# A pass over the finished instruction list moves some 60 early operations, and the last unit is finished chunk by chunk (attention + expert FFN, one core)

## The chip, the cores and the metric

One core of one Trainium2 chip runs the kernel. The metric is device time in microseconds (us) of one execution, lower is better. Engines are named as in the profile: PE (TensorE matmul; PEld its weight loads), DVE (VectorE), ACT (ScalarE), POOL (GpSimd), SP (the queue that issues the DMAs).

## The reference

x has 8 batches of 512 tokens with 256 features, all in float32. Two sandwiched layers:

```
x = x + layernorm(attn(layernorm(x)))
x = x + layernorm(ffn(layernorm(x)))

attn:  x_proj = x @ w_in.T + b_in           # 16 heads of 16
       att = softmax(q k.T / 4)             # per head, 512 x 512
       opt = einsum('blmh,blhd->blhd', att, v)
       return opt @ w_out.T + b_out
ffn:   top1 = argmax(softmax(x @ gate_W.T + gate_b))       # of 8 experts
       inter = relu(x @ wi_W.T + wi_b + lora_top1(x))      # 1024 wide, rank 4
       return inter @ wo_W.T + wo_b
```

In `opt` the sum over m concerns att alone, so the weights of each row add up to about one: what stays of a head is v times a factor from the row sums. The kernel still forms every score, its row maximum and its exponentials' sum.

## The kernel before, in words

**Precision.** float32 products are made of three matmuls on split operands: `three` (L463) multiplies high by high, high by low and low by high parts. Every operand is therefore split into a rounded high part and the rest: `split` (L297, L299, L301 the high part, L305 the low part) and, out of PSUM, `split_ps` (L360 and L382 on ACT, L367 and L373 on DVE).

**Tiles and stages.** A batch is four chunks of 128 tokens; two chunks make a unit, so there are 16 units. For a batch: `layernorm` (L390: bn_stats L397 and bn_aggr L402 on DVE; nr, the inverse deviation, on POOL at L410 and L415; the apply at L437 on POOL or L439 on DVE), transposes on PE (L454), split into xnh and xnl (L506, L513), then `project` (L520) for groups 0 and 1 of eight heads, queries and keys, into PSUM tiles psqk and from there into hl. `lay_out_k` (L543, DMAs at L556 into `rows`) and `lay_out_q` (L563, DMAs at L577 for the first unit of batch 0, L590 elsewhere) spread hl over partitions for pairs of heads. `scores` (L602) makes for each pair, chunk and head one 128x512 product (L635 for batch 0's first unit, with 64 rows; L626 elsewhere), its negative row maximum nmax on DVE (L645) and exp with row sums on ACT (L654). Five PSUM tiles hold scores. `values`, `attend` and `feed` (L908) follow per unit: v, output projection, layernorm, gate and experts, the FFN's psh and psz, and at the end z, its layernorm, the residual and the output DMA (L976, L397 to L439, L984, L989).

**What sets the order.** Nothing is emitted where it is written. `Plan.op` (L69) records each operation with an engine, a cost and the tiles it reads and writes; `Plan.order` (L103) runs a list scheduler over them with the due times in `WIN` and `PRI`, and at L1156 the finished list is emitted. Each engine then works through its own part of that list strictly in order; semaphores between engines follow from the tiles. SP's DMAs reuse eight semaphores in turn, so a DMA waits until the one eight places earlier has landed.

**What the change touches.** At the start: the x loads (L268) and weight loads (L283) on SP, four of them for wo; `warm_up` (L1009), 100 matmuls of ones into the tile psu (L1016); `first_weights` (L1043: wqk split, and bqk scaled at L1062); the layernorm of batch 0 on DVE (ln_x, L439); the weight splits wv, wout, wi, wo on POOL (L321, L297 and L305); the layernorms of batches 1 to 3 (st_x, mv_x on DVE, nr_x and ln_x on POOL); `gate_weights` (L1089: wga L1093 and L1098, lbh L1111, lbs L1116). In the list before, PE runs 46 psu, the transposes of batch 0 with 2 psu between, 20 psu, the projections and values of batch 0, 23 psu, four scores, 9 psu, and then the scores. At the end: the last unit (batch 7, chunks 2 and 3), whose layernorm and residual run on DVE (`QUICK`).

Of the kernel before, what the change touches and what calls it, by code (L numbers as in the profile page):

```python
# [17 lines left out]
P = 128  # L18
# [30 lines left out]


class Op:
    __slots__ = ("eng", "cost", "share", "lag", "fn", "urgency", "tiles", "after", "deps", "ready", "n", "group")


class Plan:
# [10 lines left out]
    def op(self, eng, cost, fn, reads=(), writes=(), holds=(), share=1.0, lag=0.0, behind=()):  # L66

        o = Op()  # L70
        o.eng, o.cost, o.share, o.lag = eng, cost, share, lag
        o.fn, o.n = fn, len(self.ops)
        o.urgency = self.at
        o.group = None
        deps = set(behind)
        for t in reads:
            deps.update(t.writers)
        for t in writes:
            deps.update(t.readers)
        deps.discard(o)  # L80
        o.deps, o.after, o.ready = len(deps), [], 0.0
        for d in deps:
            d.after.append(o)
        for t in reads:
            t.readers.append(o)
        for t in writes:
            t.writers.append(o)
        o.tiles = list(dict.fromkeys([*reads, *writes, *holds]))
        for t in o.tiles:
            t.left += 1  # L90
        self.ops.append(o)
        return o
# [89 lines left out]
def kernel(  # L182
# [59 lines left out]
    def mm(n, times=1):  # L242
        return (max(n / 2.208, 108) + 2.5) * times
# [3 lines left out]
    def const_tile(shape, dtype, name, parts=1):  # L247
        return plan.tile(const, shape, dtype, name, 1, name)
# [83 lines left out]

    ident = const_tile([P, P], F32, "ident")
    plan.op(POOL, 500, lambda: make_identity(nc, ident()), writes=[ident])
    mhalf = const_tile([P, NC], F32, "mhalf")
    fill(mhalf, -0.5)

# [49 lines left out]
                ({"B": POOL, "D": DVE, "F": ACT}[how], POOL),  # L387
            )

    def layernorm(src, sel, n, pool_, tag, bufs, name, eng=POOL, at_once=None):  # L390

        m = at_once or n
        st = plan.tile(small, [P, n, nc.vector.BN_STATS_DIM], F32, "st", 4, f"st_{name}", False)
        mv = plan.tile(small, [P, n, nc.vector.BN_AGGR_DIM], F32, "mv", 4, f"mv_{name}", False)
        for c in range(n):
            plan.op(
                DVE, 335, lambda c=c: nc.vector.bn_stats(st()[:, c, :], sel()[:, c, :]),  # L397
                reads=[src], writes=[st],
            )
        for c in range(n):  # L400
            plan.op(
                DVE, 75, lambda c=c: nc.vector.bn_aggr(mv()[:, c, :], st()[:, c, :]),  # L402
                reads=[st], writes=[mv],
            )
        few = HOW["few"]
        fe = {POOL: nc.gpsimd, DVE: nc.vector}[few]
        nr = plan.tile(small, [P, 2, n], F32, "nr", 4, f"nr_{name}", False)
        plan.op(
            few, 235 if few == POOL else 70,
            lambda: fe.tensor_scalar(nr()[:, 1, :], mv()[:, :, 1], 1.0, EPS, ALU.mult, ALU.add),  # L410
            reads=[mv], writes=[nr],
        )
        state[0].setdefault("stats", plan.op(
            POOL, 355 + 165 * n,
            lambda: nc.gpsimd.tensor_tensor(  # L415
                nr()[:, 1, :], nr()[:, 1, :], mhalf()[:, :n], ALU.pow
            ),
            reads=[nr, mhalf], writes=[nr],
        ))
        if eng == POOL:  # L420
            plan.op(
                few, 235 if few == POOL else 70,
                lambda: fe.tensor_scalar(
                    nr()[:, 0, :], mv()[:, :, 0], -1.0, 0.0, ALU.mult, ALU.add
                ),
                reads=[mv], writes=[nr],
            )
        e = nc.gpsimd if eng == POOL else nc.vector
        dsts = []
        for c0 in range(0, n, m):  # L430
            dst = plan.tile(pool_, [P, m, D], F32, tag, bufs, f"ln_{name}_{c0}")
            for c in range(c0, c0 + m):
                def apply(c=c, dst=dst, c0=c0):
                    r = nr()[:, 1, c : c + 1]
                    to, x_ = dst()[:, c - c0, :], sel()[:, c, :]
                    if eng == POOL:
                        e.tensor_scalar(to, x_, nr()[:, 0, c : c + 1], r, ALU.add, ALU.mult)  # L437
                    else:
                        e.tensor_scalar(to, x_, mv()[:, c, 0:1], r, ALU.subtract, ALU.mult)  # L439

                plan.op(
                    eng, 540 if eng == POOL else 323, apply, reads=[src, nr, mv], writes=[dst]
                )
            dsts.append(dst)
        return dsts

    def transposed(src, n, name, holds):

# [32 lines left out]
    def prepare(b):  # L481

        st = state[b]
        xh = plan.tile(work, [P, ND, L], F32R, "xnh", XNB, f"xnh_{b}")
        xl = plan.tile(work, [P, ND, L], F32R, "xnl", XNB, f"xnl_{b}")
        e = LN0 if b == 0 else POOL
        if LN4 or b == 0 and LN40:
            xns = layernorm(
                xts[b], lambda: xts[b](), NC, work, "xn", XNN, f"x_{b}", e, at_once=2
            )  # L490
        else:
            xns = []
        for h in range(2):
            if len(xns) <= h:
                xns += layernorm(
                    xts[b], lambda h=h: xts[b]()[:, 2 * h : 2 * h + 2], 2, work, "xn", XNN,
                    f"x_{b}_{h}", e,
                )
            xn = xns[h]
            ps = transposed(xn, 2, f"xn_{b}_{h}", [xh, xl])  # L500

            toks = slice(h * 2 * P, (h + 1) * 2 * P)
            how = HOW["xn"]
            plan.op(
                ACT, act(512),
                lambda ps=ps, toks=toks: nc.scalar.activation(  # L506
                    xh()[:, :, toks], ps(), AF.Identity
                ),
                reads=[ps], writes=[xh], holds=[xl],
            )  # L510
            plan.op(
                DVE, dve(512),
                lambda ps=ps, toks=toks: nc.vector.tensor_tensor(  # L513
                    xl()[:, :, toks], ps(), f32(xh()[:, :, toks]), ALU.subtract
                ),
                reads=[ps, xh], writes=[xl],
            )
        st["x"] = xh, xl

    def project(b, g):  # L520

# [386 lines left out]
    def feed(b, u):  # L908
# [9 lines left out]
        for f2 in range(NF // 2):  # L918
# [34 lines left out]
            )  # L953
            hh.append(a)
            hl.append(c)
        z = plan.tile(unit, [P, n, D], F32, "z", 1, f"z_{name}")
        psz = plan.tile(ps_w, [P, n, D], F32, "w", PB, f"psz_{name}", False)
        for i in range(n):
            cols = slice(i * P, (i + 1) * P)
            for f2 in range(NF // 2):  # L960
                plan.op(
                    PE, mm(D, 6),
                    lambda i=i, f2=f2, cols=cols: three(
                        psz()[:, i, :],
                        [hh[f2]()[:, k, cols] for k in range(2)],
                        [hl[f2]()[:, k, cols] for k in range(2)],
                        [wo_h()[:, 2 * f2 + k, :] for k in range(2)],
                        [wo_l()[:, 2 * f2 + k, :] for k in range(2)],
                        start=(f2 == 0), stop=(f2 == NF // 2 - 1),
                    ),  # L970
                    reads=[hh[f2], hl[f2], wo_h, wo_l] + ([psz] if i or f2 else []),
                    writes=[psz], holds=[z],
                )
        plan.op(
            DVE, dve(n * D),
            lambda: nc.vector.tensor_tensor(  # L976
                z(), psz(), wob_sb().unsqueeze(1).to_broadcast([P, n, D]), ALU.add
            ),
            reads=[psz, wob_sb], writes=[z],
        )  # L980
        (res,) = layernorm(z, lambda: z(), n, unit, "res", RSB, f"z_{name}", eng)
        plan.op(
            eng, pool(n * D, 1) if eng == POOL else dve(n * D),
            lambda: ve.tensor_tensor(res(), x1(), res(), ALU.add),  # L984
            reads=[x1, res], writes=[res],
        )
        plan.op(
            DMA, DMA_COST,
            lambda: nc.sync.dma_start(  # L989
                out=out[b].rearrange("(p c) d -> p c d", c=NC)[:, cs[0] : cs[0] + n],  # L990
                in_=res(),
            ),
            reads=[res], lag=DMA_DELAY,
        )

# [155 lines left out]
            during(tu, "attend" + k, attend, b, u)  # L1153
            during(tu, "feed" + k, feed, b, u)

    done = plan.order()  # L1156
    with tc.manual_schedule():
        for o in done:
            o.fn()
# [78 lines left out]
LN40 = True  # L1238
XNN = 2
W0LO = 'DVE'  # L1240
WARM = 100
XB = 4
HLB = 6
# [5 lines left out]
PB = 3  # L1249
# [65 lines left out]
```

## Time and profile before

| | us |
|---|---|
| median of 3 runs | 519.96 |
| lowest, highest | 519.34, 522.47 |
| the profiled execution | 522.59 |
| its span (first to last instruction) | 520.8 |

| engine | busy us | share of the span | instructions |
|---|---|---|---|
| PE | 495.3 | 95% | 3204 |
| PEld | 434.3 | 83% | 3204 |
| DVE | 468.6 | 90% | 1054 |
| ACT | 436.9 | 84% | 1205 |
| POOL | 390.5 | 75% | 612 |

A page of the profile shows one execution. Its part 2 cuts the span into 40 slices of 13 us; a digit is the busy share in tenths, and the row PEclk is the clock that TensorE was granted. A timeline line gives start, length, engine, line, operation, output and inputs, their shapes and the count; in brackets stands the idle time ahead of it and what ended that. The mean granted clock was 0.961. From the raw clock records, it was 0.5 from 12.60 to 16.01, from 33.08 to 56.97 and from 74.04 to 80.87 us, and once more from 493.88 to 497.29.

### The profile page before, as it was taken

Reading aid. Unit: us, or ns where it says so; the run is one execution under the profiler, and the core shown is the slowest. Engines: PE = TensorE matmul, PEld = TensorE weight load, DVE = VectorE, ACT = ScalarE, POOL = GpSimd, SP = SyncE. Lnnn points to the kernel's source line nnn. Section 1 sums busy time; section 2 is a strip of 40 time slices with the busy share of each in tenths; the row PEclk is TensorE's granted clock in tenths of the full one; section 3 lists DMA queues with packets and bytes.
Section 4 is the critical chain, followed back from the end, with each engine's and each line's share of the span. In section 5 each row is a group of like instructions: output and inputs, shape, how many; then the busy total and the mean of one; then the engine's idle time right before and its main releaser. Section 6 shows DMA issues by size and latency. Waiting matters only on the chain.

```text
span 520.8 us, 11345 instructions
## 1 busy us (share of the span) xinstructions
PE 495.3 (95%) x3204; PEld 434.3 (83%) x3204; DVE 468.6 (90%) x1054; ACT 436.9 (84%) x1205; POOL 390.5 (75%) x612
## 2 busy tenths in 40 slices
PE   7989989999999999999999999999999989998994
PEld 6955847879888988989989889988898978998994
DVE  5878899999999999999999999999999989997622
ACT  2279999998999999998999999999999979984210
POOL 8793454665889987997979997788878767887741
PEclk9875888999999999999999999999999999999998
DMA  8663253324423442243323442244223422100001
GB/s 266 223 172 77 49 141 82 89 63 109 115 50 105 110 113 66 67 131 97 98 67 114 102 97 67 61 113 109 53 65 96 128 65 69 41 21 22 1 21 40
DMA packets 41038, 46.56 MB, mean 89 GB/s; under 512 B 11310, under 2 KB 27950, under 8 KB 40976
## 3 DMA queue, kind: packets, MB, share of 16 engines
q1 hardware_dynamic: 40976, 45.84, 33.0%
q8 instruction: 26, 0.43, 0.4%
q14 instruction: 36, 0.29, 0.2%
HBM read 8.05 MB, written 4.19 MB: 24 GB/s over the span
## 4 chain that ended last, share of the span: by engine, by line
PE 62%; DVE 19%; ACT 5%; issue 3%; DMA 2%; POOL 1%; SPq 0%; POOLq 0%; ACTq 0%; DVEq 0%
PE sc L626 16%; PE psz L471 14%; PE psh L471 12%; DVE nmax L645 11%; PE psqk L471 6%; ACT sc L654 4%; PE psy L471 3%; PE psv L471 2%; PE psh L944 2%; PE sc L635 1%; DMA q<-hl 1%; PE psg L795 1%; PE pst_xn L454 1%; PE psg L798 1%; PE pst_x L454 1%
## 5 line engine op out<-in xcount | busy, mean ns | idle before, releaser
L654 ACT ACTIVATE sc<-sc,nmax 128x512 f32<-128x512 f32 x512 | 343.0, 690 | 13.3 <-DVE nmax L645 6.7
L645 DVE TENSOR_REDUCE nmax<-sc 128x1 f32<-128x512 f32 x512 | 325.4, 678 | 11.0 <-PE sc L626 6.4
L626 PE MATMUL sc<-rows,q 128*128 128x512 f32 x480 | 183.2, 424 | 8.1 <-ACT sc L654 4.1
L654 ACT ACTIVATION_READ_ACCUMULATOR sc<-sc,nmax 128x1 f32 x512 | 121.0, 236 | 0.0
L626 PEld LDWEIGHTS sc<-rows,q 128*128 128x128 f32 x480 | 88.8, 192 | 28.4 <-ACT sc L654 21.7
L471 PE MATMUL psz<-woh,hTh 128*128 128x256 f32 x256 | 73.6, 288 | 0.8 <-DVE xnl L513 0.4
L471 PE MATMUL psh<-x2h,wih 128*128 128x256 f32 x256 | 72.9, 285 | 0.0
L471 PE MATMUL psz<-wol,hTh 128*128 128x256 f32 x256 | 72.7, 284 | 0.0
L471 PE MATMUL psz<-woh,hTl 128*128 128x256 f32 x256 | 72.7, 284 | 0.0
L471 PE MATMUL psh<-x2h,wil 128*128 128x256 f32 x256 | 72.0, 281 | 0.0
L471 PE MATMUL psh<-x2l,wih 128*128 128x256 f32 x256 | 71.9, 281 | 0.0
L305 POOL TENSOR_TENSOR hTl<-full_h,hTh 128x512 fp32r<-128x512 f32 x44 | 57.0, 1295 | 2.3 <-DVE hTh L299 1.1
L471 PEld LDWEIGHTS psz<-wol,hTh 128*128 128x128 f32 x256 | 49.0, 191 | 3.7
L471 PEld LDWEIGHTS psh<-x2l,wih 128*128 128x128 f32 x256 | 48.2, 188 | 3.2
L471 PEld LDWEIGHTS psz<-woh,hTh 128*128 128x128 f32 x256 | 48.9, 191 | 2.0 <-DVE hTl L367 0.6
L471 PEld LDWEIGHTS psh<-x2h,wih 128*128 128x128 f32 x256 | 48.2, 188 | 1.2 <-DVE y L761 0.2
L471 PEld LDWEIGHTS psz<-woh,hTl 128*128 128x128 f32 x256 | 48.9, 191 | 0.2 <-POOL hTl L305 0.2
L471 PEld LDWEIGHTS psh<-x2h,wil 128*128 128x128 f32 x256 | 48.1, 188 | 0.0
L305 POOL TENSOR_TENSOR hl<-full_qk,hl 128x512 fp32r<-128x512 f32 x28 | 36.4, 1301 | 1.2
L382 ACT ACTIVATE full_h<-psh 128x512 f32<-128x512 f32 x44 | 26.4, 606 | 10.5 <-PE psh L944 10.0
L297 POOL TENSOR_SCALAR hl<-full_qk 128x512 fp32r<-128x512 f32 x28 | 17.4, 623 | 21.8 <-ACT full_qk L382 21.4
L471 PE MATMUL psqk<-xnh,wqkh 128*128 128x512 f32 x64 | 27.6, 431 | 0.0
(128 smaller groups left out, 1043.5 us busy)
## 6 DMA issues: line engine op xcount, KB each, us to landing
rows<-hl SPq DMA_DIRECT2D x128, 128.0 KB, 2.6
q<-hl SPq DMA_DIRECT2D x480, 32.0 KB, 2.0
out<-ln_z SPq DMA_DIRECT2D x16, 256.0 KB, 2.2
xt<-in_x SPq DMA_DIRECT2D x7, 512.0 KB, 3.8
wi<-in_wi SPq DMA_DIRECT2D x4, 256.0 KB, 6.8
wo<-in_wo SPq DMA_DIRECT2D x4, 256.0 KB, 6.7
q<-hl SPq DMA_DIRECT2D x16, 64.0 KB, 2.1
xt<-in_x SPq DMA_DIRECT2D x2, 256.0 KB, 2.7
```

The source lines that it names most:

```text
L297: nc.gpsimd.tensor_scalar(pick_hi(), pick(), 1.0, 0.0, ALU.mult, ALU.add)
L305: e.tensor_tensor(pick_lo(), pick(), f32(pick_hi()), ALU.subtract)
L382: lambda: nc.scalar.activation(full(), flat(ps()), func, **kw()),
L454: nc.tensor.transpose(ps()[:, dc, c * P : (c + 1) * P], src()[:, c, dc * P : (dc + 1) * P], ident(),)
L471: nc.tensor.matmul(ps, w, xx, start=start and i == 0, stop=stop and i == len(terms) - 1)
L626: nc.tensor.matmul(sc(), q()[:, e, cols], k(), start=True, stop=True)
L635: nc.tensor.matmul(sc(), q()[rows, 0, cols], k()[rows], start=True, stop=True)
L645: lambda sc=sc, nmax=nmax: nc.vector.tensor_reduce(nmax(), sc(), AX.X, ALU.max, negate=True),
L654: lambda sc=sc, nmax=nmax, esum=esum, i=i, h=h: nc.scalar.activation(sc(), sc(), AF.Exp, bias=nmax(), accum_out=esum()[:, i, h : h + 1]),
L795: nc.tensor.matmul(psg()[:, :, c], xh()[:, dc, cols], wga_hl()[:, dc], start=dc == 0, stop=False)
L798: nc.tensor.matmul(psg()[:, 0, c], xl()[:, dc, cols], wga_hl()[:, dc, 0], start=False, stop=dc == ND - 1,)
L944: nc.tensor.matmul(ps()[:, i, :], lbs()[:KL, fs], axs()[:KL, : n * P], start=False, stop=i == 1,)
```

## The change

Two parts.

*The last unit.* psz is two PSUM tiles, one for each chunk, and the 8 groups of six matmuls are emitted in the order (chunk, f2) = (0,0) (1,0) (0,1) (1,1) (0,2) (0,3) (1,2) (1,3) and no longer chunk by chunk. Each chunk then has its own bias sum, statistics, nr and output DMA. The apply is split: the mean is subtracted in place on DVE as soon as mv is there (`apart`), and the scaling by nr and the residual are one scalar_tensor_tensor. The step of chunk 0 is set behind mv of chunk 1. For the other 15 units the code makes the same instructions as before.

*The start.* `settle` takes the finished list and moves operations behind others:

- DVE: bqk's scaling behind the last ln_x of batch 0; both lbh behind the second xnl; statistics of batches 1 to 3 between the hl steps and between maxima; both lbs and wga between maxima (behind the maxima of the 8th, 14th and 20th score).
- POOL: wi's last two parts behind nr of batch 1; nr of batch 2 and 3 behind their statistics and ln_x; wo's four parts behind ln_x of batch 3 and behind hl_1_0_0. A new one-element operation `calm` reads the last ln_x of batch 0, and all POOL work that stood between nr of batch 0 and that point follows it.
- SP: q and rows of the first pairs alternate (q_0, rows_0, q_1, rows_1, ...), and the four wo loads stand behind rows_1; before, six q DMAs led and wo was loaded ahead of the x of later batches.
- PE: of 100 psu matmuls the first 30 stay.

ACT's order is unchanged. The core of the diff:

```diff
+        behind(of(DVE, "ln_x_0_2")[-1], of(DVE, "bqk"))
+        lbh = of(DVE, "lbh_0", "lbh_512")
+        behind(of(DVE, "xnl_0")[-1], lbh)
+        st2, turns = of(DVE, "st_x_2"), of(DVE, "hl_0_0_0", "hl_0_0_1", "hl_0_1_0")
+        st1, maxes = of(DVE, "st_x_1"), of(DVE, "nmax_0_0_1_1", "nmax_0_2_0_1")
+        behind(turns[0], st1[:2])
+        behind(turns[1], st1[2:] + of(DVE, "mv_x_1"))
+        behind(turns[2], st2[:2])
+        behind(maxes[0], st2[2:] + of(DVE, "mv_x_2"))
+        behind(of(DVE, "nmax_0_2_0_1")[0], of(DVE, "st_x_3", "mv_x_3"))
+        lbs = of(DVE, "lbs")
+        behind(of(DVE, "nmax_0_1_1_1")[0], lbs[:1])
+        behind(of(DVE, "nmax_0_3_0_1")[0], lbs[1:])
+        behind(of(DVE, "nmax_0_4_1_1")[0], of(DVE, "wga"))
...
+        behind(of(DVE, "mv_x_1")[-1], nr[1] + [wih[2], wil[2], wih[3], wil[3]])
+        behind(of(DVE, "mv_x_2")[-1], nr[2])
+        behind(of(POOL, "ln_x_2_2")[-1], nr[3])
+        behind(
+            [o for o in of(POOL, "ln_x_3_0")][-1], [woh[0], wol[0], woh[1], wol[1]]
+        )
+        behind(of(POOL, "hl_1_0_0")[-1], [woh[2], wol[2], woh[3], wol[3]])
+        calm = Op()
+        calm.eng, calm.mark = POOL, None
+        calm.fn = lambda: nc.gpsimd.tensor_scalar(
+            calm_sb(), state[0]["xn"]()[:, 1, :1], 1.0, 0.0, ALU.mult, ALU.add
+        )
+        last = of(DVE, "ln_x_0_2")[-1]
+        early = [o for o in done[done.index(nr[0][-1]) + 1 : done.index(last)] if o.eng == POOL]
+        behind(last, early)
+        done.insert(done.index(last) + 1, calm)
...
+        rows = []
+        for p in range(NP):
+            if p < X1B:
+                rows += of(DMA, f"q_0_{p}")
+            rows += of(DMA, f"rows_0_{p}")
+            if p == 1:
+                rows += of(DMA, "wo_0", "wo_1", "wo_2", "wo_3")
+        behind(turns[1], rows)
...
+        extra = of(PE, "psu")[FIRST:]
+        return [o for o in done if o not in extra]
+
+    done = settle(plan.order())
```

and of the last unit:

```diff
+        if apart:
+            plan.op(
+                DVE, dve(n * D),
+                lambda: nc.vector.tensor_scalar(
+                    sel(), sel(), mv()[:, 0, 0:1], None, ALU.subtract
+                ),
+                reads=[src, mv], writes=[src],
+            )
+            return lambda: [nr]
...
+            steps.sort(key=lambda s: (s[1] + (1 if s[1] == 2 and s[0] else 0) if s[1] < 3 else 3 + s[0], s[0]))
+            steps = [s for s in steps if s != (1, 2)]
+            steps.insert(steps.index((0, 3)) + 1, (1, 2))
...
+                nr, r = r, z if i0 else res
                 plan.op(
+                    DVE, dve(D),
+                    lambda sel=sel, r=r, nr=nr: nc.vector.scalar_tensor_tensor(
+                        r()[:, sel], z()[:, sel], nr()[:, 1, 0:1], x1()[:, sel],
+                        op0=ALU.mult, op1=ALU.add,
                     ),
+                    reads=[x1, z, nr], writes=[r],
                 )
```

## The prediction, made before the changed kernel was run

> **What bounds the kernel now.** I read the page's part 2 first (who is busy when, and the granted TensorE clock), then the busy time by stage, then the timeline of the first 30 us and of the last 8 us, because the list of instructions per engine shows that only these two places change: between about 60 and 507 us the order is the same on every engine.
>
> ```profile
> PE   7989989999999999999999999999999989998994
> PEclk9875888999999999999999999999999999999998
> 57.00:72.00 15.00, 14.13 (x71) 10.41 (x69) 14.37 (x28) 14.81 (x42) 9.91 (x12) 1.00 0.27 64
> 90.00:150.00 60.00, 58.67 (x389) 51.85 (x388) 58.83 (x132) 56.53 (x159) 41.05 (x63) 1.00 0.34 88
> 150.00:300.00 150.00, 149.07 (x1007) 134.04 (x1006) 145.05 (x338) 142.53 (x397) 132.62 (x205) 1.00 0.37 95
> ```
>
> The three number lines are: stretch, length, busy PE, PEld, DVE, ACT, POOL, granted clock, DMA share, GB/s. From 90 us on PE is busy 98 to 99% of the time, with DVE and ACT close behind. Nothing there can be gained by the change, but whatever the head gives is carried to the end unchanged. So the question is how much earlier the steady part starts, and how much shorter the last chain is.
>
> ```profile
> 6.48 0.17 DVE L1062 TENSOR_SCALAR bqk<-bqk 128x2 f32<-128x2 f32 x1 [1.72 <-DMA bqk<-in_bqk]
> 7.64 1.03 POOL L415 TENSOR_TENSOR nr_x<-nr_x,mhalf 128x4 f32<-128x4 f32 x1
> 8.71 3.88 DVE L439 TENSOR_SCALAR ln_x<-xt,mv_x,nr_x 128x256 f32<-128x256 f32 x4 [1.21 <-POOL nr_x L415]
> 13.20 3.87 PE L1016 MATMUL psu<-ones 128*128 128x256 f32 x20
> 20.50 4.39 SPq L577 DMA_DIRECT2D q<-hl  x6
> 28.25 0.73 PE L635 MATMUL sc<-rows,q 64*128 64x512 f32 x4
> 28.79 7.27 DVE L645 TENSOR_REDUCE nmax<-sc 128x1 f32<-128x512 f32 x12 [1.29 <-PE sc L635]
> ```
>
> Times are start and length. The reader is to see four brakes: DVE waits for bqk, whose result nobody needs yet; ln_x takes 3.88 us for four pieces, while the same form takes 0.74 for two at 516.31, where POOL is idle; warm-up matmuls stand ahead of the first projection; six q transfers go ahead of rows on SP, so the first score starts only at 28.25.
>
> ```profile
> 513.50 0.69 DVE L976 TENSOR_TENSOR z<-psz,wob 128x512 f32<-128x512 f32 x1 [4.37 <-PE psz L471]
> 514.23 0.75 DVE L397 BATCH_NORM_STATS2 st_z<-z 128x6 f32<-128x256 f32 x2
> 515.56 0.71 POOL L415 TENSOR_TENSOR nr_z<-nr_z,mhalf 128x2 f32<-128x2 f32 x1
> 517.08 0.69 DVE L984 TENSOR_TENSOR ln_z<-ln_y,ln_z 128x512 f32<-128x512 f32 x1
> ```
>
> Behind the last matmul (513.39) stands a serial chain of two chunks, 4.38 us long, until 517.77.
>
> **The head, step by step.**
> 1. bqk moved behind ln_x. mv_x starts when st_x ends (3.35 + 1.41 = 4.76) instead of 6.55. The POOL step nr_x then waits for the memsets of q (until 5.64), and the pow of 1.03 us ends at 6.98 instead of 8.67. wqkl (DVE, 0.66) needs wqkh from ACT at 6.56; it meets the pow on the way and ends about 7.5 (blocked ones in this trace end 0.53 after POOL's instruction: lbs at 23.98 + 1.10, POOL's woh until 24.55). ln_x starts at 7.5 instead of 8.71.
> 2. calm. It reads the last ln_x on POOL, so POOL's weight splits start behind it. ln_x then costs 4 x 0.33 = 1.3 us, not 3.88, and ends at 8.8 instead of 12.6. POOL idles for 7.0 to 8.8, but starts the splits only 0.2 to 1 us later than before (8.66), as its pow ended 1.7 earlier.
> 3. xnl before lbh. wqkl to 9.5, xnl_0 to 10.2, xnl_1 to 10.8 (0.65 each). The second matmul of the first projection, which reads xnl, starts at 10.85 instead of 17.14: 6.3 us.
> 4. Warm-up: 70 of 100 psu are gone (0.11 us each at the full clock, 7.6 us). Those that stood ahead of psqk held it 0.5 us past xnl (16.39 to 16.91), already counted; the 32 between psqk and the scores covered a wait for rows, and cost nothing.
> 5. The projections last 8.43 us (17.14 to 25.57), so 10.85 to 19.3 at the full clock. hl_1_1 needs ACT 0.65 and DVE 0.7 behind it, where DVE is now free: 20.7. The first maximum stands right behind it on DVE: 20.7 instead of 28.79, **-8.1**. The transfers must keep up: hl_0_0 is done by 13.8; q_0's second transfer reuses the semaphore of the third xt load, which I put at 16 (it landed at 19.36, behind 1.05 MB of wo that now comes later, at some 400 GB/s: 2.6 less, and it starts earlier); rows_0 goes out at 16.3 and 17.0 and lands 2.6 later, 19.6. Just in time.
> 6. Given back on DVE. Work that ran before the first maximum now stands between maxima: st_x_2 and mv (0.98), lbs (0.66 plus a blocked part, some 1.1 each), st_x_3 and mv (1.65), wga (0.4). Counted on DVE with 0.606 per maximum, xnl of the second batch ends 14.6 us behind the first maximum; before it was 40.33, that is 11.5, and PE got to the projection that needs it 12.6 behind (41.41). So **+2.0**. At the fifth pair a score buffer is then late by **+0.5**; later DVE, 2.42 busy per 3.06 us, catches up.
> 7. SP. The four wo loads stand between rows_1 and q_2: 4 x 0.55 = 2.2 us. SP issues without a break from 20.50 to 45, so it starts 6 us earlier and is 3.7 us earlier from q_2 on. q_3 to q_7 landed 2.3 to 3.4 us before their scores, and SP's waits on PE and POOL between 38 and 72 (3.4 us in all) shrink with it: covered up to a gain of about 6. wo on POOL (four pairs of 1.93) falls into POOL's gaps at 42.3 to 47.3 and 49.3 to 55.9: nothing. nr_2 now waits for mv_x_2; ln_x of batch 1 is then ready 6 us behind the first maximum, and PE asks for it 6.5 behind it: nothing.
> 8. The clock. The gate is judged in stretches of 3.41 us. After 70.63 to 74.04, with five matmuls of 512 columns (5 x 0.213 = 1.07 us, 31%), the clock goes to 0.5; 12.60 to 16.01, four fifths full at half clock, opens it; 50.15 to 53.56, about half full, does not. With 30 psu PE has its last one at 7.0 and the first projection at 10.85. The stretch 5.78 to 9.19 then holds 11 psu (1.2 us, 35%): at the edge, and its phase may differ in each run. Closed at full 3.41 us it costs at most 1.7 us; a half-filled stretch that does not open it adds up to 0.8. Bounds 0 and 2.5; I take **+1.5**, nearer to closed, since most placings of the stretches leave one of them less than 30% full.
>
> The Trainium skill (TensorE: Matmul & The Clock Gate, "Why this matters for your kernels") warns against gaps of over about 3 us, as one idle window halves the clock. By that rule the gap of 3.9 us always closes the gate, and the sum would take 1.7 to 2.5 here; the rows put the edge at a third of a window's matmuls, so 0 is possible too.
>
> Head: -8.1 + 2.0 + 0.5 + 1.5 = **-4.1**. Bounds -6.5 to -1.5.
>
> **The tail.** Chunk 0 ends 12 matmuls (1.42 us) ahead, its sum, statistics and subtraction run below PE. Behind the last matmul remain, for one chunk: z 0.33, statistics 0.33, mv 0.1, nr 0.19 plus 0.1 hand-over, pow (1.03 for four columns, 0.71 for two, so about 0.55), hand-over 0.1, last step 0.36: 2.1. res of chunk 0 and the subtraction stand on DVE meanwhile; res reads two SBUF tensors and may hold POOL's nr by 0.3 to 0.6. So 2.1 to 2.9 instead of 4.38; I take 2.7, **-1.7** (bounds -1.4 to -2.3). The interleaved psz order has the same 48 matmuls; its hTl are ready (last one 509.13, asked for at 511). The extra DMA issue (0.33) lies beside DVE. The 2 to 3 us of the last transfer stay.
>
> The Trainium skill (SBUF — State Buffer, "SBUF: two separate sides") calls this shared port an exclusive lock held for the whole instruction. By it the tail is -1.4 to -1.7; without a lock -2.3. The rows at 8.71 and 23.98 speak for it.
>
> **Sum.** -4.1 - 1.7 = -5.8. The profiled execution took 522.59 (span 520.8, 1.8 around it) and would take 516.8. It lies 2.6 above the median, so for the median 519.96 - 5.8 = **514.2**.
>
> **The rivals.**
> - The gate stays open in the gap: -5.8 - 1.5 = -7.3, 512.7; with less given back on DVE down to 510. For it: 35% against 31%. Chance 0.22.
> - DVE becomes the path: all 5.2 us of work moved behind the first maximum stays on it (DVE is 14.4 of 15 busy at 57 to 72), so step 6 is 5.2 and not 2.5: 516.9. Against: 4 us of idle DVE at 36 to 57. Chance 0.17.
> - calm does not hold POOL off: ln_x stays near 3.9, +2.4: 516.6. Against: it reads what the last ln_x writes. Chance 0.05.
> - Slower: the gate does not open in the projections at all, 8.43 x 0.83 = +7.0 instead of 1.5, and opens one stretch (1.7) later than before at 57: -5.8 + 5.5 + 1.7 = +1.4, 521.4. It decides from 7.3 / 1.7 = 4.3 closed stretches more than before. Against: the projections fill a stretch without a gap, as psu did at 12.60. Chance 0.06.
>
> **How the numbers follow.** My forecast, 514.2, has chance 0.50. The range 510.0 to 517.6 holds the first three cases and calm's. A measurement of this kernel tells about 1% (5.2 us, 514.76) from no change; of the likeliest case some six tenths lie below it, with the open gate 0.30 + 0.22 = 0.52 and a little of the third: 0.54. Slower by over 1% only if the closed gate goes on for longer: 0.05. The rest, 0.41, is within 1%.
>
> **What would show it.** ln_x four pieces in 1.3 to 1.5 us at 7.5; second psqk at 10.9; first maximum at 20.7 to 22.5; second batch's first projection at 36 to 38 instead of 41.41; a closed stretch between 9 and 16; last DVE step 2.1 to 2.9 behind the last matmul. A first score that waits for rows, or maxima that wait for lbs for over 1.3 us, would prove steps 5 to 7 wrong.

## The result, and the profile after

| | before | changed |
|---|---|---|
| median of 17 runs each, side by side | 519.87 us (518.62 to 523.42) | 517.01 us (513.44 to 518.92) |
| ratio, 95% interval | | 0.9928 [0.991, 0.9946] |
| profiled execution | 522.59 us | 513.44 us |
| its span | 520.8 us | 511.6 us |

The change makes the kernel 0.7% faster, 2.8 to 4.7 us by the interval. The interval leaves no change out, but the gain is under the 1% at which the prediction drew its line. The forecast was -5.8. The two profiled executions lie 9.2 us apart, since the one before is among the slowest of its kernel and the one after is the fastest of its own. Read by itself this pair would have been taken for a larger gain than forecast; where the 9.2 us come from has to be split first.

Page of the changed kernel, part 2 (busy tenths in 40 slices, granted clock):

```profile
PE   7769989999999999999999999999999999998995
PEclk9955879999999999999999999999999999999999
```

Busy time by stretch of the changed kernel (columns as in the prediction):

```profile
57.00:72.00 15.00, 13.43 (x59) 8.73 (x57) 15.00 (x31) 15.00 (x43) 8.25 (x11) 0.96 0.39 90
150.00:300.00 150.00, 149.06 (x1010) 134.51 (x1009) 145.41 (x336) 142.67 (x397) 132.52 (x207) 1.00 0.39 96
```

The steady part is what it was. In the head the clock falls to half earlier (the third digit of PEclk is 5, before it was 7), and PE is less busy in slices 2 and 3 (7 and 6, before 9 and 8).

Timeline of the changed kernel, head (start, length; in brackets the idle time before, and what ended it):

```profile
7.77 1.38 DVE L452 TENSOR_SCALAR ln_x<-xt,mv_x,nr_x 128x256 f32<-128x256 f32 x4
...
11.16 0.50 PE L486 MATMUL psqk<-xnl,wqkh 128*128 128x512 f32 x1 [0.22 <-DVE xnl L528]
...
15.79 1.97 SPq L593 DMA_DIRECT2D q<-hl  x2
...
21.11 0.74 PE L651 MATMUL sc<-rows,q 64*128 64x512 f32 x4 [1.32 <-DMA rows<-hl]
21.65 2.48 DVE L661 TENSOR_REDUCE nmax<-sc 128x1 f32<-128x512 f32 x4 [0.34 <-PE sc L651]
21.67 2.01 SPq L284 DMA_DIRECT2D wo<-in_wo  x4
23.72 1.19 SPq L593 DMA_DIRECT2D q<-hl  x2
...
29.55 1.22 PE L651 MATMUL sc<-rows,q 64*128 64x512 f32 x4 [4.22 <-DMA rows<-hl]
30.35 1.29 DVE L661 TENSOR_REDUCE nmax<-sc 128x1 f32<-128x512 f32 x2 [2.12 <-PE sc L651]
...
37.28 0.79 PE L486 MATMUL psqk<-xnh,wqkh 128*128 128x512 f32 x1
```

The first maximum comes at 21.65 instead of 28.79, 7.1 us earlier. The second batch's first projection comes at 37.28 instead of 41.41, only 4.1 earlier. Between them stand the four wo loads on SP, and behind those the third pair's scores wait 4.22 us for rows.

Timeline of the changed kernel, end:

```profile
505.63 0.28 PE L486 MATMUL psz<-woh,hTl 128*128 128x256 f32 x1
...
506.00 0.42 DVE L1011 TENSOR_TENSOR z<-psz,wob 128x256 f32<-128x256 f32 x1
506.22 0.56 POOL L417 TENSOR_TENSOR nr_z<-nr_z,mhalf 128x1 f32<-128x1 f32 x1
...
507.30 0.48 DVE L1028 SCALAR_TENSOR_TENSOR res<-z,nr_z,ln_y 128x256 f32<-128x256 f32 x1 [0.20 <-issue]
507.46 0.74 POOL L417 TENSOR_TENSOR nr_z<-nr_z,mhalf 128x1 f32<-128x1 f32 x1
...
508.24 0.48 DVE L1028 SCALAR_TENSOR_TENSOR z<-z,nr_z,ln_y 128x256 f32<-128x256 f32 x1 [0.19 <-POOL nr_z L417]
```

The last matmul ends at 505.91, DVE's last step at 508.72: 2.81 us instead of 4.38.

**Splitting the 9.2 us of the profiled pair.** DVE's 544 maxima (512 of scores, 32 of the gate's) come in the same order in both kernels, so the k-th of one can be set against the k-th of the other. The 1st is 7.1 us earlier, the 33rd 2.8, the 73rd 3.1, the 401st 3.4. Two jumps follow, at 366 us (0.7) and at 424 us (1.9), where PE of the kernel before waited for q transfers (timeline, the second of them):

```profile
423.79 0.71 PE L626 MATMUL sc<-rows,q 128*128 128x512 f32 x2 [2.21 <-DMA q<-hl]
```

The changed kernel waited 0.8 us in all for the same transfers. Then the kernel before had its clock at half from 493.88 to 497.29, the changed one had not: 1.4 more between the last maximum and the last matmul, and the tail's 1.57 on top. Neither the wait at 424 nor that closed stretch is the change's: over all fourteen profiles of this study the clock closes near 490 in eight, and the stretch from the 481st to the 489th maximum takes from 6.9 to 9.5 us, whatever the head was. So the pair shows 3.1 for the head, 1.6 for the tail, and some 4.5 us of chance.

### The profile page after: what moved, and what is told of

It is laid out like the page before. It is cut to its first block, busy times and chain, and to the rows that moved or that the text cites. A ratio compares the mean times of both kernels' runs of the same rounds, so it can differ in the third digit from the quotient of the medians.

```text
span 511.6 us, 11203 instructions
## 1 busy us (share of the span) xinstructions
PE 483.8 (95%) x3134; PEld 423.7 (83%) x3134; DVE 467.3 (91%) x1056; ACT 436.4 (85%) x1205; POOL 390.1 (76%) x615
## 4 chain that ended last, share of the span: by engine, by line
PE 62%; DVE 24%; ACT 4%; DMA 3%; issue 2%; SPq 2%; POOL 1%; POOLq 0%; ACTq 0%; DVEq 0%
PE sc L642 16%; PE psz L486 14%; DVE nmax L661 13%; PE psh L486 12%; PE psqk L486 7%; PE psy L486 3%; ACT sc L670 3%; PE psv L486 3%; PE psh L960 2%; DVE st_x L399 2%; PE sc L651 1%; DMA q<-hl 1%; DMA rows<-hl 1%; DVE hTh L300 1%; PE pst_x L469 1%
## 5 line engine op out<-in xcount | busy, mean ns | idle before, releaser
L670 ACT ACTIVATE sc<-sc,nmax 128x512 f32<-128x512 f32 x512 | 342.6, 689 | 17.1 <-DVE nmax L661 10.6
L642 PEld LDWEIGHTS sc<-rows,q 128*128 128x128 f32 x480 | 88.7, 192 | 25.7 <-ACT sc L670 18.7
```

The costliest lines, as they stand in the source:

```text
L642: nc.tensor.matmul(sc(), q()[:, e, cols], k(), start=True, stop=True)
L670: lambda sc=sc, nmax=nmax, esum=esum, i=i, h=h: nc.scalar.activation(sc(), sc(), AF.Exp, bias=nmax(), accum_out=esum()[:, i, h : h + 1]),
```

## The experiments

The theory after the result: the tail gives what was forecast; the head gives much less than forecast, because what the first maximum gains is given back between the first maximum and about 51 us. Rivals for what takes it back: wo in front of rows_2 on SP; DVE, with the work moved behind the first maximum; PE at half the clock. And a rival for the medians: the clock gate, which in most executions closes in the gap ahead of the first projection, where the profiled one kept it open.

All readings in one table. "1st", "9th", "33rd" and "73rd" are starts of those maxima in the profiled execution (us), the ratio is to the kernel before, run beside it.

| kernel | 1st | 9th | 33rd | 73rd | median | ratio, 95% interval |
|---|---|---|---|---|---|---|
| before | 28.79 | 33.58 | 54.30 | 87.58 | 519.87 | |
| changed | 21.65 | 30.35 | 51.46 | 84.50 | 517.01 | 0.9928 [0.991, 0.9946] |
| e1 tail only | 29.92 | 34.71 | 54.59 | 87.89 | 518.55 | 0.9965 [0.9942, 0.9988] |
| e2 head only | 22.55 | 32.12 | 53.25 | 87.30 | 520.01 | 0.9985 [0.9957, 1.0012] |
| e3 wo behind rows_2 | 22.25 | 28.77 | 51.91 | 84.94 | 516.22 | 0.9915 [0.9888, 0.9943] |
| e4 psu in the gap | 21.69 | 30.15 | 51.26 | 84.29 | 515.50 | 0.9913 [0.9887, 0.9938] |
| e5 changed, again | 21.88 | 31.68 | 52.79 | 86.22 | 516.31 | 0.9936 [0.9909, 0.9963] |
| e6 DVE work early | 21.90 | 30.87 | 51.97 | 84.94 | 517.44 | 0.9939 [0.991, 0.9969] |
| e7 e6 and e3 | 21.18 | 26.78 | 50.45 | 83.97 | 516.30 | 0.9919 [0.9891, 0.9947] |
| e8 clock kept open | 21.70 | 30.80 | 51.43 | 84.38 | 517.45 | 0.995 [0.9929, 0.9972] |
| e9 wo by ACT | 24.54 | 31.05 | 52.13 | 85.96 | 516.82 | 0.9941 [0.9911, 0.997] |
| e10 e9 and e6 | 24.92 | 29.71 | 51.57 | 84.58 | 517.31 | 0.9941 [0.9914, 0.9969] |
| e11 no calm | 21.30 | 30.26 | 52.12 | 85.56 | 517.99 | 0.9946 [0.992, 0.9973] |
| e12 three relieved | 22.23 | 29.33 | 51.02 | 84.40 | 517.55 | 0.9933 [0.991, 0.9955] |

**Tail alone (e1).** The changed kernel with the list of the kernel before in the head.

```diff
-    done = settle(plan.order())
+    done = plan.order()
```

> This is the changed kernel with the list of the kernel before it in the head (nothing settled anew, 100 psu); only the last unit goes chunk by chunk. Additive theory: the chain behind the last matmul is 2.8 us as in the profiled changed kernel instead of 4.38, so the median falls by 1.4 to 1.7 us (ratio 0.997) and the first maximum stays at 28.8. Rival: the two DMAs of half the size and the interleaved order of psz lose it elsewhere, so the median falls by under 0.5.

Measured 0.9965, which is -1.8 us of 520.54 (-3.0 to -0.6); the chain behind the last matmul is 2.82 us. The additive theory holds; the rival lies just outside the interval. The first maximum came at 29.92 and not at 28.8: the old head, too, differs by 1.1 us from one profile to the next.

**Head alone (e2).** The settled list, the last unit as before.

```diff
-        last = b == B - 1 and u == len(units(b)) - 1
+        last = False
```

> The settled list and 30 psu, with the last unit as in the kernel before. Theory that the profiled pair shows the whole: maxima of the steady part are 3.05 us earlier there, so the median falls by 2.5 to 3.3 us (ratio 0.994). Rival, the clock gate: the profiled execution of the changed kernel had the clock open through the gap between 7 and 10.4 us by luck; in most others it closes there, and the median falls by only 1 to 2 us, with the fastest of the executions 2 us or more below the median.

Measured 0.9985, -0.8 us (-2.2 to +0.6), which by itself is not told from no change. The theory that the profiled pair shows the whole (-2.5 to -3.3) is out. The rival's -1 to -2 lies in the interval, but its reason does not show: the profile has the clock open through the gap, as the changed kernel's had. Its first maximum is 0.9 later than the changed kernel's, and the third pair's wait for rows is longer:

```profile
31.33 1.22 PE L651 MATMUL sc<-rows,q 64*128 64x512 f32 x4 [5.09 <-DMA rows<-hl]
```

Between 71.45 and 81.69 the clock is at half for three stretches instead of two; a further 1.0 us goes there (73rd maximum against 57th).

**wo behind rows_2 (e3).**

```diff
-            if p == 1:
+            if p == 2:
                 rows += of(DMA, "wo_0", "wo_1", "wo_2", "wo_3")
```

> The four wo loads go out behind rows_2 instead of ahead of q_2. Theory 'wo holds rows_2': the scores of the third pair wait 4.22 us for rows in the changed kernel, and DVE idles 2.12 us for them; rows_2 is issued some 2 us earlier and lands 2.6 instead of 3.8 us behind its issue, so the wait falls under 1 us, the maxima behind it come 1.5 to 2.1 us earlier, and so does the end (median 515 to 515.6 against 517.0 of the changed kernel). Rival 'DVE or POOL is the path anyway': the 2.1 us are given back by ln_x of the second batch (POOL) or by later pairs whose rows now stand behind wo; the second batch's first projection stays at 37.3 and the median at 517.

Timeline of this kernel:

```profile
26.97 2.27 PE L651 MATMUL sc<-rows,q 64*128 64x512 f32 x4 [1.04 <-DMA rows<-hl]
33.77 0.80 PE L651 MATMUL sc<-rows,q 64*128 64x512 f32 x2 [3.48 <-ACT sc L670]
```

The wait does go to 1.04 us, and the 9th maximum comes 1.6 earlier. Then PE waits 3.48 for a score buffer, as st_x_3 on DVE stands between the third pair's maxima, and the 33rd maximum is where it was. The wait was real; moving wo behind one more pair gained nothing that the profile or the interval shows (515 to 515.6 was expected, 516.22 measured).

**psu in the gap (e4).** 37 psu first, 6 behind each group of four transposes.

```diff
-        extra = of(PE, "psu")[FIRST:]
+        psu = of(PE, "psu")
+        pst = [o for o in done if o.eng == PE and o.mark.startswith("pst_xn")]
+        behind(pst[0], psu[37:43])
+        behind(pst[1], psu[43:49])
+        extra = psu[49:]
```

> 37 psu ahead of the first transposes, 6 behind the first four, 6 behind the second four, so that no stretch of 3.41 us between 6 and 16 us has under 40% of matmuls. Gate theory: the clock is open in the gap in every execution, the median falls by 0.8 to 1.7 us below that of the changed kernel (515.3 to 516.2 against 517.0) and the executions scatter less. Rival: the clock was open there in most executions, the median stays within 0.5 us of 517.0.

0.9913 against 0.9928 and 0.9936 of the changed kernel: the intervals overlap, the profile's maxima agree within 0.2 us. The median, 515.50, is what the gate theory expected, but its interval holds the changed kernel too; median and scatter do not separate the two theories. What separates them is the count of profiles: with 30 psu the clock, once open (at 5.1 to 7.9 us), stayed open to 16 us and beyond in ten of eleven (this kernel not counted), and closed only in e9, from 11.89 to 15.30.

**The changed kernel again (e5).** Control, unaltered.

> The changed kernel once more, unaltered, as control for the three beside it and for its scatter. Theory 'small head': its profiled execution was a lucky one; the median is again 516.5 to 517.5 and a second profile shows the first maximum up to 0.9 us later than 21.65, or a clock that closes for longer between 70 and 82 us. Rival: the profiled one is typical, the median comes out near 514.

516.31, ratio 0.9936: a small head again, and a less lucky profile. Its third pair waits longer for the same rows:

```profile
30.89 1.22 PE L651 MATMUL sc<-rows,q 64*128 64x512 f32 x4 [5.47 <-DMA rows<-hl]
```

The same head list was thus profiled three times unaltered (changed, e5, e2), and its 73rd maximum came at 84.50, 86.22 and 87.30, mean 86.0; the old one twice (before, e1), at 87.58 and 87.89, mean 87.7. That is -1.7 us for the head, and fits the medians: -3.7 in all less -1.8 for the tail is -1.9. The head alone, measured in e2, is -0.8; with intervals of about 1.4 us to either side these agree, but none of them fixes the head to better than that.

**DVE work early (e6, e7).** The rest of st_x_2, mv_x_2 and the first lbs go into DVE's idle time ahead of the last hl; e7 also has wo behind rows_2.

```diff
-        behind(turns[2], st2[:2])
-        behind(maxes[0], st2[2:] + of(DVE, "mv_x_2"))
+        lbs = of(DVE, "lbs")
+        behind(turns[2], st2 + of(DVE, "mv_x_2") + lbs[:1])
...
-        behind(of(DVE, "nmax_0_1_1_1")[0], lbs[:1])
```

> The second half of st_x_2, mv_x_2 and the first lbs (1.98 us of DVE) go ahead of the last hl, into DVE's idle time of 2.35 us there, instead of between the maxima; wo stays ahead of q_2. Theory 'DVE is the path': the maxima of the second pair come 1.0 us earlier, but the third pair waits for its rows as before, so only up to 1 us is left at the second batch's first projection and at the end (516 to 516.5). Rival 'PE at half clock is the path from 36 us': nothing is left at the end.

> The same, and wo behind rows_2 as in the run before. Theory 'DVE is the path once rows come in time': maxima stand back to back from the first to the eighth pair's, the second batch's first projection starts 2 us earlier than 37.3 and the median is 515 to 515.5. Rival 'PE at half clock': from 36 to 54 us PE is busy 98% at a clock of 0.5 whatever comes before; the gain at 36 is kept there (PE's fixed work only starts earlier), but if the clock opens in fixed steps it comes out in steps of 3.41 us of half clock, that is 0 or 1.7 us. Rival 'score buffers': DVE's st_x_3 between the maxima of the third pair stops ACT and PE again, and all is given back (517).

e6: from the 1st to the 33rd maximum DVE's busy time falls from 25.9 to 24.3 us, its idle time rises from 3.9 to 5.8; nothing gained. The third pair's rows came no earlier, so that DVE only stood idle longer in front of them (4.0 us up to the 9th maximum, 2.1 in the changed kernel). The rival's 'nothing is left' is what was measured; its reason, PE at half clock, is looked at in e8. e7: the 9th maximum is 3.6 us earlier than in the changed kernel, the 33rd 1.0, the 73rd 0.5, and the median, 516.30, is not the 515 to 515.5 of the theory. Now the fourth pair waits for its q, which SP issues behind wo and rows_3 (waits of PE, total, times, longest):

```profile
PE sc L651 <- DMA q<-hl: 3.5, 1, 3.5
```

**Clock kept open (e8).** Matmuls of psu's kind ahead of each score step of the first unit, into the score's own tile.

```diff
                 def products(scs=scs, q=q, k=k, cols=cols, p=p):
+                    rhs = ones().unsqueeze(1).to_broadcast([P, 2, P])
+                    for _ in range(8 if p < 3 else 5):
+                        nc.tensor.matmul(scs[0]()[:, : 2 * P], ones(), rhs, start=True, stop=True)
                     for e, sc in enumerate(scs):
```

> The changed kernel with 8 matmuls of psu's kind ahead of each of the first six score steps and 5 ahead of the other ten of the first unit, written into the score's own tile before the score itself; nothing else differs. Theory 'the closed clock costs in the head': with 128-row matmuls in each stretch the clock stays open from 23 to 54 us, PE is no longer full from 36 to 54, and the maxima at the end of that stretch come 1.5 to 3 us earlier (median 514 to 515.5). Rival: DVE, 87% busy there, is the path just as well, or the wait for rows_2 closes the clock all the same; the extra matmuls, 0.21 us each at half clock, then cost up to 5 us (517 to 522).

Page of this kernel:

```profile
PEclk9999979999999999999999999999999999999999
```

The clock is open from 5.22 to 70.07 instead of closed from 23.05 to 53.77, and the 33rd maximum moves by less than 0.1 us. That alone does not show that the half clock is free, because the added matmuls use up PE time. The stretch has to be cut at the 21st maximum. Busy time from the 9th to the 21st and from there to the 33rd in the changed kernel (columns as in the prediction):

```profile
30.35:42.26 11.91, 11.37 (x29) 6.05 (x28) 11.87 (x26) 9.45 (x26) 8.67 (x13) 0.50 0.53 129
42.26:51.46 9.20, 9.20 (x22) 4.87 (x21) 7.46 (x14) 8.38 (x24) 5.62 (x6) 0.50 0.25 58
```

From the 21st to the 33rd in e8, and the one stretch in which the clock was open in e2, which has the same head and no added matmuls:

```profile
42.71:51.43 8.72, 8.08 (x43) 5.38 (x42) 7.45 (x14) 8.26 (x24) 5.62 (x6) 1.00 0.24 56
40.73:44.14 3.41, 2.60 (x9) 1.25 (x9) 3.38 (x8) 3.07 (x9) 2.99 (x3) 1.00 0.30 75
```

Up to the 21st maximum DVE is the bound: it has no idle time from the third pair on, and the 9th to the 21st take 11.9 us at half clock (changed, e2, e5) and at full clock (e8). In e2's open stretch PE only waits more, for score buffers that ACT has not yet freed. From the 21st to the 33rd PE is busy throughout in the changed kernel, and there the half clock does cost: 9.20 us, and 9.19 or 9.20 in all ten profiles of the settled list with the clock at half, against 8.72 in e8 and in e12. So it costs at least 0.5 us; e8 does not show that at its 33rd maximum because its 9th came 0.45 later. The theory's 1.5 to 3 us are not there, and the median, 517.45, is at the low end of where the rival put it.

**wo off SP (e9, e10).** The four loads issued by ScalarE behind its third hl; e10 with the DVE edit of e6.

```diff
-            DMA, DMA_COST, lambda: nc.sync.dma_start(out=t()[:rows], in_=src), writes=[t],
+            DMA, DMA_COST,
+            lambda: (nc.scalar if name.startswith("wo_") else nc.sync).dma_start(
+                out=t()[:rows], in_=src
+            ),
+            writes=[t],
...
-            if p == 1:
-                rows += of(DMA, "wo_0", "wo_1", "wo_2", "wo_3")
         behind(turns[1], rows)
+        behind(of(ACT, "hl_0_1_0")[0], of(DMA, "wo_0", "wo_1", "wo_2", "wo_3"))
```

> The changed kernel with the four wo loads issued by ScalarE, behind its third hl, where it idles from 16.1 to 19.8 us; SP's list is otherwise the same, 2.05 us shorter ahead of q_2. Theory 'SP is the path': SP issues from the first q (15.8 us) to 97 us at 0.64 us for each transfer without a break, in this kernel and in every other; the changed kernel gained 4.7 us at the first q and lost 2.05 to wo behind it, and that is the 2.9 us that stayed. Without wo on SP the q and rows transfers from q_2 on go out 2.0 us earlier, rows_2 does not wait, the maxima of the steady part come 1.5 to 2 us earlier and the median is 515 to 515.5. Rival 'DVE is the path': only the 2.1 us that DVE waits for rows_2 go, the fourth and later pairs give most of it back, as they did with wo behind rows_2 (median 516.3 to 517). Rival: wo's 1 MB shares the DMA engines with q_0 and rows_0, the first score is late by 0.5 to 1.5 us.

> The same, with the 1.98 us of DVE work (rest of st_x_2, mv_x_2, first lbs) ahead of the last hl. Theory 'SP and DVE stand side by side, each within 1 us of the path': both are relieved by 2 us, and the maxima of the fifth pair and behind it come 2 to 3 us earlier than in the changed kernel; median 514 to 515. If SP alone is the path, this is no faster than the kernel beside it.

Timeline of e10, and DVE's share of the stretch from the 1st to the 21st maximum in e9:

```profile
23.78 1.19 SPq L597 DMA_DIRECT2D q<-hl  x2
24.12 1.22 PE L655 MATMUL sc<-rows,q 64*128 64x512 f32 x4 [4.21 <-DMA rows<-hl]
24.92 6.07 DVE L665 TENSOR_REDUCE nmax<-sc 128x1 f32<-128x512 f32 x10 [3.36 <-PE sc L655]
...
24.54:42.94 18.40, 16.37 (x37) 8.12 (x36) 18.36 (x41) 15.02 (x42) 12.62 (x20) 0.53 0.58 144
```

The rival of shared DMA engines struck harder than put: rows_0 lands some 3 us later, and SP then waits, so that q_2 goes out at 23.78, as with wo on SP (23.72). In e9 the clock also closed from 11.89 to 15.30, and ACT's third hl stands at 17.40 instead of 15.37. So these runs do not test a shorter SP queue. The medians, 516.82 and 517.31, miss what both theories put (515 to 515.5, 514 to 515); e9's is where the rival 'DVE is the path' put it. They show something else: in e10 the first maximum is 3.3 us later than in the changed kernel and the 33rd is 0.1 later. With the later start no wait comes between; DVE works from the 1st to the 21st maximum without idle time, 18.4 us in e9 and 17.45 in e10, and most of what was lost at the first maximum is made good by the 21st.

**No calm (e11).**

```diff
-        behind(last, early)
-        done.insert(done.index(last) + 1, calm)
```

> The changed kernel without the small POOL instruction that holds POOL's weight splits until the last ln_x. Prediction's step 2: ln_x takes 3.9 us instead of 1.37 for four pieces, the second matmul of the first projection comes 2 to 2.5 us later than 11.16, and so does the first q transfer (17.8 to 18.3) and, if SP is the path, the steady part by the same 2 to 2.5 (median 519 to 519.5). Rival: POOL's splits only move into a place where they block lbh instead, less than 1 us is lost at the second matmul.

Timeline of this kernel:

```profile
7.06 1.38 DVE L452 TENSOR_SCALAR ln_x<-xt,mv_x,nr_x 128x256 f32<-128x256 f32 x4
8.67 0.92 POOL L298 TENSOR_SCALAR wvh<-wv 128x512 fp32r<-128x512 f32 x1 [1.64 <-DMA wv<-in_wv]
```

Step 2's side missed: ln_x takes 1.38 without calm too, and the second matmul of the projection starts at 10.56. The rival's 'less than 1 us' holds, but not for its reason: lbh is not held longer (2.38 us for two, 2.97 in the changed kernel). POOL waits for wv until 8.67 by itself, and ln_x, started earlier, is over by 8.44. What made ln_x short is its earlier start; calm only insures it. The median, 517.99, is not the 519 to 519.5 that was expected either.

**Three relieved at once (e12).** e6's and e8's edits, and wo issued by POOL behind the fourth ln_x of the second batch (e9's edit with nc.gpsimd and that place).

> Three relieved at once: 1.98 us of DVE work ahead of the last hl, wo off SP (issued by POOL in its gap behind the fourth ln_x of the second batch), and the clock kept open by matmuls of psu's kind ahead of the scores of the first unit. Each alone left the 33rd maximum where it was (51.4 to 52.1 us). Theory 'several queues stand side by side': with all three relieved it comes 1.5 to 3 us earlier (48.5 to 50), the median is 514 to 515.5. Rival 'the rest is the score pipeline itself' (maximum, exp, next score through five buffers, ACT at 0.66 us each): no more than 1 us, as in the run with two of them (50.5), median 516 to 517.5. POOL's four issues in front of its ln_x may cost up to 2 us at the second batch's first projection.

The 33rd maximum comes 0.4 earlier than in the changed kernel, and that is the open clock behind the 21st, which comes at 42.29 (42.26 in the changed kernel). The rival's number holds (no more than 1 us); the median, 517.55, is at the edge of its 516 to 517.5. SP's relief was used up at the sixth pair (timeline, SP and PE):

```profile
33.80 1.51 SPq L597 DMA_DIRECT2D q<-hl  x2
36.41 1.19 SPq L576 DMA_DIRECT2D rows<-hl  x2
37.12 0.59 PE L658 MATMUL sc<-rows,q 64*128 64x512 f32 x2 [1.43 <-DMA q<-hl]
```

SP stands still for 1.1 us ahead of 36.41 and is then as late as in the changed kernel (37.65 at the first transfer for the second unit, 37.41 there). No kernel of the study is faster than the changed one beyond the intervals.

## Why the prediction was right and wrong

The direction held, and the time lies inside the range (510.0 to 517.6), near its upper end. Of the two likely classes the likelier one (faster by over 1%, 0.54) did not come; within 1%, which came, had 0.41. The middle was 2 to 3 us too low, and all of that is in the head.

1. **bqk moved.** mv_x at 4.93 (4.76 said), pow to 7.03 (6.98), ln_x at 7.77 (7.5). Right.
2. **calm.** ln_x takes 1.38 (1.3). Size right, cause wrong: e11.
3. **xnl first.** Second matmul at 11.16 (10.85). Right.
4. **psu at nothing.** Nothing speaks against it: with 19 more (e4) the maxima come within 0.2 us of the changed kernel's.
5. **First maximum at 20.7.** 21.65, 21.88 and 22.55 in three profiles. The first scores wait 1.25 to 1.45 us for rows, which the prediction named as a sign against this step. hl_1_1 would have held the maximum to 21.3 anyway: PE's projections end at 19.8 instead of 19.3, as they start 0.3 later, and ACT's and DVE's parts and hand-overs take 1.5.
6. **Given back on DVE +2.0 and +0.5.** The size holds where it can be read by itself. From the 1st to the 21st maximum the kernel before takes 16.2 us (15.4 in e1): DVE works 14.0 and stands idle 2.2 (1.4). With the changed list it works some 18.5. In e9, where it has no idle time on the way, the stretch takes 18.4: 2.2 to 3.0 given back, as the work moved there, 4.4 us, first fills the idle time that was there before.
7. **wo on SP "covered".** This is the step that failed. SP sends off rows_2 at 24.96 instead of 27.50, 2.5 us earlier and not 3.7, while the first maximum is 7.1 earlier. The third pair's scores then wait 4.2, 5.5 and 5.1 us for them in the three profiles, and DVE stands idle for them 2.1, 3.2 and 3.0. So the 1st to the 33rd maximum take 29.8, 30.9 and 30.7 us instead of 25.5 (24.7 in e1): 4.3 to 5.4 given back, not 2.5, and all of it by the 21st. The second rival (all 5.2 us of moved work stay on the path, 516.9) has the measured number, and half of the mechanism: from the third pair's rows to the 21st maximum DVE is the path (idle 0.04 of 11.91 us), but part of the moved work fills old idle time, and the rest of the loss is the wait for rows. Bringing those rows forward by itself (e3, e7) put other waits in its place: DVE's idle time up to the 21st maximum is 1.5 and 2.7 us there.
8. **Clock +1.5.** Mis-sized: the gate closed in the gap in one of eleven profiles, so 0.1 to 0.2 on the mean. The end of the range at 0 was the case, and this error was luck for the forecast: it made up for about a third of what steps 5 to 7 lost. With this term right and the others as they were, the sum would have been some 1.3 us further off. The 35% worked out for the first stretch was 31% in the changed kernel's profile (5.99 to 9.40), and the clock stayed at 1.0; a stretch of 31% at 67.42 to 70.84 was followed by half the clock. The share of matmuls alone does not draw the line. By the rule of the Trainium skill (TensorE: Matmul & The Clock Gate, "Why this matters for your kernels"), that an idle window halves the clock, the gap of 3.9 us that was forecast would have closed it each time. Measured it is 3.0 us in the changed kernel (7.43 to 10.44); the transposes at 8.23 stand in it, and the runs do not say whether they count.

**Tail -1.7.** -1.57 by the trace (2.81 us behind the last matmul, 2.7 said), -1.8 [-3.0, -0.6] by e1. The number is right, its parts less so: the second pow takes 0.74 with res over it and the first 0.56, so res holds POOL by 0.2 and not by 0.3 to 0.6. The other 0.5 above the bare sum of 2.1 is that one chunk's DVE steps and hand-overs cost more than was put (z 0.42 for 0.33, the last step 0.48 for 0.36). The exclusive lock of the Trainium skill (SBUF — State Buffer, "SBUF: two separate sides") put the tail at -1.4 to -1.7. The measured tail lies there and the longer pow agrees in kind, but the pow makes only 0.2 us of it.

**The sum with the measured terms:** first maximum -6.8 (mean of three against 28.79), given back up to the 33rd +5.0 (30.5 against 25.5) and from there to the 73rd +0.2: -1.6 against before's own profile, -1.7 against the mean of the two old heads; with the tail's -1.6, -3.2 to -3.3. The ratio says -2.8 to -4.7.

**What stays open.** Which resource holds the 21st maximum. It comes between 42.1 and 42.9 us in nine of the twelve profiles of the settled list (41.26, 43.58 and 44.05 in the others), from first maxima between 21.2 and 24.9; behind it nothing differs up to the 33rd but the clock. DVE's work fills 17 to 19 us of the way there, the rest is waits. The wait for rows_2 (e3), 1.6 us of DVE work (e6), the half clock (e8) and three things together (e12) were taken away, and a first maximum 3.3 us later was put in; the 33rd moved by 1.0 at most where the unaltered list scatters by 1.8. Each relief shows the next wait: score buffers behind st_x_3 (e3), q_3 behind wo on SP (e7), SP at the sixth pair (e12). SP issues a transfer each 0.64 us almost without a break from the first q to 97 us in both kernels, so it is a candidate, but no run shortened its queue past the sixth pair, and moving q and rows to a second queue was not tried.

## What to carry to other kernels

A gain at the front of a pipeline counts only at the point where the steady part begins: set the k-th instruction of a long series of one kernel against the k-th of the other, and price the stretch between on each queue by itself: the work moved into it less the idle time that was there, and the waits for transfers that now stand behind others. Idle time can be spent once only; here the moved work took it, and the wait for rows came on top. Where the queues are all nearly full and the bound changes twice within 30 us (rows, DVE, PE), a wait that the profile names can be removed without gain, as the next lies right behind it. And a single profiled execution can differ from its own kernel's median by more than the change is worth: profile the same list twice before reading a gain of 1%.

## What the runs showed of the hardware that was not expected

- A half TensorE clock under a PE that is 100% busy was worth only 0.5 us of 9.2: the 21st to the 33rd maximum take 9.19 to 9.20 us in ten profiles at half clock, and 8.72 in both with the clock at 1.0 (e8, e12, with added matmuls).
- 1 MB issued from a second queue while SP's transfers are in flight delays those: the first pair's rows, issued at 18.0 in e10, let PE start at 24.12; the changed kernel, with its rows issued at 17.85, started at 21.11.
- POOL and ACT issue a 256 KB load in about 0.6 us each (2.38 us for four on POOL in e12, 2.49 on ACT in e9), SP in 0.5 (2.01).
- The clock closes near 490 us in eight of fourteen profiles of nearly the same instructions. From the last maximum to the last matmul it is then 18.6 to 18.7 us, otherwise 17.1 to 17.2.
